# More buffers in each stage of the last group, and stretched pauses while two groups are emitted side by side

## The chip, the cores and the metric

The kernel runs on one core of a Trainium2 chip. The metric is the device time of that core in microseconds (us), smaller being better. The engines named below are TensorE (PE in the profile, with PEld for its weight loads), VectorE (DVE), ScalarE (ACT), GpSimd (POOL) and the queues that start transfers (SP is the one that starts nearly all of them here).

## The reference

The input x has 16 images of 32 channels and 128 by 128 pixels, all float32. Four layers follow one another, and each has the same frame; `_gn` is a group norm with 16 groups of two channels, without scale or shift:

```python
x = x + L0(_gn(x))      # a recurrence over the 128 columns: a row LSTM, 32 hidden channels
x = x + L1(_gn(x))      # adder convolution
x = x + L2(_gn(x))      # Hartley mode mixing
x = x + L3(_gn(x))      # edge operators and a small U-shaped stack of convolutions
```

L1 quantises its input and its 3x3 weights to 8 bits and takes, for each of 32 output channels, minus the sum of |patch − w| over all 288 taps.

L2 is this, with `dht2d` the Hartley transform along both axes (real minus imaginary part of the Fourier transform):

```python
xm = dht2d(x)[:, :, :32, :32]
z = einsum('bixy,ioxy->boxy', xm, yeven) + einsum('bixy,ioxy->boxy', flip(xm), yodd)
out = zeros((b, 32, 128, 128)); out[:, :, :32, :32] = z
return dht2d(out) / (128 * 128)
```

L3 applies five edge operators (Sobel, Scharr, Laplace, Roberts, Prewitt) to every channel with reflected borders. Each of the five results is normalised over all channels and pixels of its image. The 160 channels then go through this chain:

```python
y = maxpool2(conv3x3(edges, conv1)); y = maxpool2(conv3x3(y, conv2))
y = maxpool2(conv3x3(y, conv3));     y = conv3x3(y, conv4)
y = conv3x3(deconv2x2(y, deconv1), conv5)
y = conv3x3(deconv2x2(y, deconv2), conv6)
y = conv3x3(deconv2x2(y, deconv3), conv7)
return x_in * y                       # x_in: L3's normalised input
```

## The kernel before

The work goes in four groups of four images; four images times 32 channels fill the 128 partitions. The tensors between the layers (`x2` before L2, `x3` before L3, the modes `xm_d`, the mixed modes `z_d`, all in HBM) are written by one stage and read again by the next. `stage0` does the LSTM and takes the first 880 us. `rest` (from line 441) does everything else.

**Stage 1 and the weave.** `Differences.run` is the adder convolution. VectorE and ScalarE take the differences (lines 705 and 702), and TensorE sums them (line 592). It lasts until 5981 us. The layers L2 and L3 of groups 0, 1 and most of group 2 run inside it as a background: the class `After` holds them as one Python generator, and the class `Weave` steps this generator. The generator yields numbers. A positive number is TensorE's planned time of what was just emitted. A negative one is a pause: the weave emits nothing more of this generator until that much planned time has gone by. `SUMMED` is a wait of 4.5 us in the phase described next. `later(us, step)` puts a step off to a planned time; `done(v)` runs such a step at once if it has not run yet, since what follows needs it. All this happens while the program is written: the pauses set the order in which instructions are emitted, and nothing on the chip waits for a clock. In stage 1, `keep_order` then fixes that order on every engine.

**The drain.** When stage 1's emission is through, `end`, a copy of `After`, is made for group 3 (the last). It has the right side of SBUF, where stage 1's memory is free now, and four PSUM banks of its own. `drain` (line 403) then steps the two generators, what is left of group 2 and all of group 3, always the one with the lesser planned time, and when one has ended it goes on with the other, which is then `alone`. Each engine runs its instructions in its order; waits for data and for free buffers come from the tiles. Here `keep_order` is not applied, so the scheduler can still move instructions.

A tile pool with n buffers under one name lets n tiles of that name be alive; the next one waits until the oldest has been read for the last time. The same number decides here how many loads the code issues ahead. These are the stages of `After.work` for one group, with their lines:

- `forward`, line 974. Eight tiles `xh` of 1 MB (half an image's channels each) are loaded from `x2` (line 992), four of them ahead. VectorE takes the group means off (`centred`, line 1014). TensorE does the first transform (line 1061), transposes (line 1076) and does the second (line 1031); VectorE copies in between (lines 1065, 1020, 1035), and the modes `xm` go to HBM (line 1041).
- `modes`, line 1105. Per image the modes come back twice, as `xs` and flipped as `xw` (line 1114; four small loads), and VectorE adds the flipped ones (lines 1121 and 1128). This step is put off by 24 us.
- `mixing`, line 1139. Eight tables `mix` of 1 MB (line 1136), three ahead, and 512 small products on TensorE (line 1149); the results `z` go to HBM (line 1173).
- `back`, line 1176. `z` comes back (line 1198). Sixteen residual tiles `xr2` of 0.5 MB (line 1191), four ahead. TensorE does the inverse transforms (lines 1212 and 1257), VectorE adds the residual and takes its statistics (lines 1235 and 1237), and the sum goes to `x3` (line 1241).
- `frames` and `statistics`, lines 1280 and 1320. A ring of two frames `xp`, each 20 rows of the group's 128 planes, loaded in halves of 0.64 MB (line 1299) and normalised by ScalarE (lines 1305 to 1312). From eight frames TensorE builds Gram matrices (line 1345). VectorE multiplies these by five tables `gm` (loads in lines 1333 and 1412) and sums, 20 pairs of instructions (lines 1405 and 1406), which gives the variances of the five edge operators.
- `first_layers`, line 1445. Ten fold tables `v` (line 1458), three ahead, are scaled by these variances and added into one set of 3x3 weights `wf` (lines 1471 and 1473): conv1 with the five operators folded in.
- `conv1`, line 1603. The same frames are loaded again; the bias product (line 1617) comes first, then the borders (line 1633) and the main products (line 1661), and pooling.
- `small_layers`: conv2 to conv4 (TensorE line 1509, pooling on VectorE line 1586, the results' copy on ScalarE line 1600), and the deconvolutions, each composed with the convolution after it (lines 849 and 874).
- `last`, line 1717. Four units, each with a residual tile `xr` of 2 MB (line 1731; a ring of two), TensorE's last composed convolution (line 849), VectorE's scale and multiply-add (lines 1789 and 1752), and the stores to the output (line 1768).

At 5981 us group 2 stands in its Gram stage and group 3 at its beginning. In the profile, group 2's conv1 starts at 6202, its `last` runs from some 6720 to 6945; group 3's conv1 is alone from 6945 to 7035, and its small layers and `last` go to 7226.

Of the kernel before, what the change touches and what calls it, by code (L numbers as in the profile page):

```python
# [299 lines left out]
class Weave:  # L300
# [10 lines left out]
    def __init__(self, work):  # L311
# [3 lines left out]
        self.draining = self.alone = False  # L315
        self.finished, self.count, self.put_off, self.for_act, self.ends = -1, 0, [], [], {}

    def later(self, us, step):
        self.count += 1
        v = self.base + us, self.count, step  # L320
        self.put_off.append(v)
        return v
# [36 lines left out]
    def step(self):  # L359
# [16 lines left out]
        elif v < 0:  # L376
            wait = -v
        else:
            us = v
# [23 lines left out]
def drain(*weaves):  # L403

    live = list(weaves)
    for w in live:
        w.draining = True
    while live:
# [4 lines left out]
        if us is None:  # L413
            live.remove(w)
            for w in live:
                w.alone = True
# [24 lines left out]
def rest(nc, tc, cst, sel16, bias, m1, r1, a, d, out):  # L441


    with ExitStack() as ctx:
# [14 lines left out]
        end.spare = bg  # L459
        end.weave = Weave(end.work([NG - 1]))  # L460
# [442 lines left out]
class After:  # L903


    def __init__(self, nc, tc, side, sm, ps, cst, bias, a, d, stat, out):
        self.nc, self.tc, self.side, self.ps, self.cst, self.bias = nc, tc, side, ps, cst, bias
        self.a, self.d, self.stat, self.out = a, d, stat, out
        self.spare, self.banks = None, 0
        store = [d["up"][i] for i in range(3)]  # L910
# [63 lines left out]
    def forward(self, g):  # L974

        nc, tc, cst, d, weave = self.nc, self.tc, self.cst, self.d, self.weave
        x2, xm_d, z_d = d["x2"], d["xm"], d["z"]
        with self.pool("t_m") as mp:
# [6 lines left out]
            with self.pool("t_t") as tp, ExitStack() as rows:  # L985
                xp = rows.enter_context(self.pool("t_x", 4))
# [8 lines left out]
                xh = [load(n) for n in range(4)]  # L995
# [30 lines left out]
                def second(n):  # L1026
# [6 lines left out]
                    def out():  # L1033
                        xm = tp.tile([128, 4, M1], F32, name="xm", bufs=2)
# [45 lines left out]
                for n in range(10):  # L1080
                    if n < 7:
                        centred(n + 1)
                    if n < 8:
                        yield first(n)
                        if n + 4 < 8:
                            xh.append(load(n + 4))
# [10 lines left out]
                wp = rows.enter_context(self.pool("t_w", 3))  # L1097
                wt = [self.weights(wp, i) for i in range(3)]
# [6 lines left out]
    def modes(self, g, b, pool, xs, steps):  # L1105

        nc, weave, xm_d = self.nc, self.weave, self.d["xm"]
        xw = pool.tile([128, 16, 32], F32, name="xw", bufs=2)
# [30 lines left out]
    def mixing(self, g, xs, wp, wt):  # L1139
# [5 lines left out]
        for ky in range(M1):  # L1145
# [13 lines left out]
            if ky % 4 == 3 and 8 < ky < M1 - 1:  # L1159
# [16 lines left out]
    def back(self, g, load):  # L1176
# [3 lines left out]
        x2, x3, z_d = d["x2"], d["x3"], d["z"]  # L1180

        with self.pool("t_z") as zp_, self.pool("t_r", 4) as rp:
# [18 lines left out]
            for n in range(4):  # L1201
# [28 lines left out]
            def take_out(n, pf):  # L1230
# [9 lines left out]
                def store():  # L1240
                    nc.sync.dma_start(rows(n)(x3), xr[n])
                    ready[n + 4] = weave.later(6.0, lambda: reload(n + 4)) if n < 12 else None

                ready[n + 4] = weave.later(4.0, store)
# [26 lines left out]
            weave.later(7.0, lambda: [load(ch, half) for ch in range(2) for half in range(2)])  # L1271
# [8 lines left out]
    def frames(self, g, pool):  # L1280
# [5 lines left out]
        ring = [pool.tile([128, 20, W + 4], F32, name=f"xp{i}") for i in range(2)]  # L1286
        for t in ring:
            nc.vector.memset(t[:, :, 0], 0.0)
            nc.vector.memset(t[:, :, W + 3], 0.0)

        def parts(ch, half):
# [3 lines left out]
            return ring[ch % 2], lo, hi, ring[ch % 2][:, off : off + hi - lo, 2 : W + 2]  # L1295
# [673 lines left out]
```

## Time and profile before

| what | us |
|---|---|
| median of 3 runs | 7219.93 (7215.45 to 7227.18) |
| profiled execution, its own time | 7227.78 |
| its span in the profile | 7226.0 |
| `stage0` | 0 to 880 |
| stage 1, with the background | 880 to 5981 |
| drain | 5981 to 7226 |
| TensorE busy in stage 1 / in the drain | 4049.7 of 5101 / 960.1 of 1245 |
| VectorE busy in stage 1 / in the drain | 4739.3 of 5101 / 432.6 of 1245 |
| ScalarE busy in stage 1 / in the drain | 4801.5 of 5101 / 267.1 of 1245 |

The table's stretches come from the profile's busy times between two instants. In the listings below, a line such as `L1121` is a line of the kernel before, `out<-in` are tile names, and `<-` after a time names what ended the wait. In an order of time, the columns are the start in us, the duration, the engine (SPq is SP's queue), the line, the operation and its tiles; a bracket at the end holds the idle time before it. In a list of waits, the three numbers are total us, times, and the longest. A matmul's record can be missing here and there, and what is busy need not be at its peak.

### The profile page before, as it was taken

The page shows a single profiled execution, that of the slowest core. Times are in us where ns is not written, and L with a number is a line of the kernel's source. Part 1 is how long each engine was busy: PE and PEld are TensorE (multiplying, and loading weights), DVE is VectorE, ACT ScalarE, POOL GpSimd, SP SyncE. Part 2 cuts the span into 40 slices and gives each one's busy share as a digit, 9 for nine tenths or more (in the row PEclk, how much of TensorE's full clock was granted, in tenths as well). Part 3 has the DMA queues.
Part 4 walks back from the last instruction along what each step waited for, and adds up shares of the span by engine and source line. Part 5 has one row for each costly group of instructions (what it writes and reads, how often), then busy time and mean ns, then how long its engine had stood idle before and what let it go on. Part 6 is the DMA issues. An engine that isn't in the chain of part 4 may idle for free. (4 is left out here: it accounts for less than half of the span.)

```text
span 7226.0 us, 271421 instructions
## 1 busy us (share of the span) xinstructions
PE 5620.8 (78%) x127740; PEld 3002.2 (42%) x127740; DVE 5845.7 (81%) x7095; ACT 5502.0 (76%) x3100; POOL 52.1 (1%) x31
## 2 busy tenths in 40 slices
PE   4778567778877776998877786999775775797896
PEld 3666333333434342333334342333332443544574
DVE  7787699999989988999999998999997994234224
ACT  2555399999999988999999998999997992121222
POOL 0000000000000000000000000000000000000000
PEclk9899789999988898999989998999888997798897
DMA  8664211111132432221343343121243245352324
GB/s 310 228 205 148 79 64 57 53 58 50 44 108 85 140 100 72 62 76 43 76 121 109 109 122 99 60 66 51 64 122 89 79 128 140 95 157 83 87 58 104
DMA packets 374319, 722.57 MB, mean 100 GB/s; under 512 B 50896, under 2 KB 219856, under 8 KB 362320
## 3 DMA queue, kind: packets, MB, share of 16 engines
q1 hardware_dynamic: 372768, 704.58, 32.1%
q8 instruction: 999, 16.37, 1.0%
q14 instruction: 120, 0.98, 0.0%
q10 hardware_dynamic: 432, 0.64, 0.0%
HBM read 507.28 MB, written 164.32 MB: 93 GB/s over the span
## 5 line engine op out<-in xcount | busy, mean ns | idle before, releaser
L702 ACT ACTIVATE d_act<-q,neg 128x8192 f16<-128x8192 f16 (+1 forms) x631 | 4463.7, 7144 | 241.5 <-PE acc L592 192.6
L705 DVE TENSOR_SCALAR d_dve<-q,qw 128x8192 f16<-128x8192 f16 (+1 forms) x1673 | 3857.3, 2361 | 183.3 <-PE acc L592 141.1
L592 PE MATMUL acc<-d_dve,sel 128*32 128x512 f16 x26768 | 1863.1, 401 | 571.7 <-DVE d_dve L705 519.3
L592 PEld LDWEIGHTS <-sel 128*32 128x32 f16 x36864 | 1026.9, 100 | 2219.2 <-issue 1563.9
L1661 PE MATMUL acc<-xp,wf 32*32 32x512 f32 x25600 | 1034.1, 619 | 31.8 <-issue 26.5
L592 PE MATMUL acc<-d_act,sel 128*32 128x512 f16 x10096 | 725.0, 409 | 345.3 <-ACT d_act L702 333.6
L1661 PEld LDWEIGHTS acc<-xp,wf 32*32 32x32 f32 x25600 | 425.0, 104 | 401.1 <-issue 319.0
L622 PE MATMUL acc<-q,zero 128*32 128x512 f16 x7248 | 520.0, 399 | 0.0
L207 PE MATMUL pg<-h,wb 64*64 64x20 f32 (+15 forms) x4096 | 395.5, 319 | 105.7 <-DVE h L256 64.4
L1600 ACT ACTIVATE y<-pooled,b 32x128 f32<-32x128 f32 x488 | 195.1, 400 | 367.8 <-DVE pooled L1586 361.4
L849 PE MATMUL acc<-y,u_conv 32*32 32x256 f32 (+1 forms) x9728 | 356.2, 461 | 78.4 <-issue 49.3
L1305 ACT ACTIVATE xp<-xp,shift,stats 128x1280 f32<-128x1280 f32 (+1 forms) x128 | 182.9, 1434 | 276.4 <-DMA xp<-x_d 265.4
L244 ACT ACTIVATE gt<-pg,bias 128x20 f32<-128x20 f32 (+15 forms) x1024 | 316.8, 375 | 79.7 <-PE pg L207 72.8
L207 PE MATMUL pg<-e,wb 64*64 64x20 f32 (+15 forms) x4096 | 353.1, 315 | 16.5 <-DVE e L260 5.4
L207 PEld LDWEIGHTS pg<-h,wb 64*64 64x64 f32 x4096 | 248.2, 153 | 140.3 <-DVE h L256 90.0
L622 PEld LDWEIGHTS <-zero 128*32 128x32 f16 x7248 | 218.4, 101 | 201.8 <-issue 44.5
L207 PE MATMUL pg<-xn,wb 64*64 64x28 f32 (+61 forms) x4096 | 284.8, 303 | 11.6 <-ACT gt L244 3.8
L207 PEld LDWEIGHTS pg<-e,wb 64*64 64x64 f32 x4096 | 251.3, 156 | 92.5 <-DVE e L260 62.9
L1345 PE MATMUL acc<-xp 32*64 32x204 f32 (+3 forms) x8576 | 243.1, 343 | 33.9 <-ACT xp L1311 26.0
L255 ACT ACTIVATE th<-c 128x20 f32<-128x20 f32 (+15 forms) x256 | 81.3, 320 | 235.0 <-DVE c L253 233.6
L849 PEld LDWEIGHTS acc<-y,u_conv 32*32 32x32 f32 x9728 | 171.1, 110 | 189.8 <-issue 126.5
L1789 DVE TENSOR_SCALAR s<-acc,l_ms,l_one 128x512 f32<-128x512 f32 x128 | 101.4, 817 | 164.7 <-PE acc L849 164.7
(212 smaller groups left out, 4255.1 us busy)
## 6 DMA issues: line engine op xcount, KB each, us to landing
xr<-x_d SPq DMA_DIRECT2D x192, 512.0 KB
xp<-x_d SPq DMA_DIRECT2D x112, 640.0 KB
q<-q_d SPq DMA_DIRECT2D x32, 2145.0 KB
x_d<-xr SPq DMA_DIRECT2D x128, 512.0 KB
x_in<-in_x_dram SPq DMA_DIRECT2D x16, 2048.0 KB
res<-in_x_dram SPq DMA_DIRECT2D x64, 512.0 KB
xn<-in_xs_dram SPq DMA_DIRECT2D x64, 512.0 KB
xn<-xn SPq DMA_DIRECT2D x128, 256.0 KB
```

What stands on the lines that cost most here:

```text
L207: nc.tensor.matmul(bank[c][q][64 * pair : 64 * pair + 64, :, :width], wb[half, 4 * kind + KIND[q]].rearrange("p b o -> p (b o)"), v[half], ...
L244: nc.scalar.activation(gt[:, q, :, :n], bank[c][q][:, :, :n], AF.Tanh if q == G else AF.Sigmoid, bias=bias[:, KIND[q] : KIND[q] + 1],)
L592: self.nc.tensor.matmul(acc[k][32 * j : 32 * j + 32, :], self.sel16[:, i // 9, :], d[:, row : row + 4, c : c + W], start=first, stop=last,)
L622: self.nc.tensor.matmul(acc[k][32 * j : 32 * j + 32, :], self.zero, q[:, :4, :W], start=False, stop=False)
L702: nc.scalar.activation(dst, src, AF.Relu, bias=self.neg[:, i : i + 1])
L705: nc.vector.tensor_scalar(dst, src, self.qw[:, i : i + 1], 0.0, ALU.subtract, ALU.max)
L849: nc.tensor.matmul(acc[blk][32 * j : 32 * j + 32, o : o + rows * n], t[part, 4 * par + tap, :], src[part, top : top + rows, left : left + ...
L1305: nc.scalar.activation(v, v, AF.Identity, bias=self.shift3, scale=self.stats3[:, 1])
L1345: nc.tensor.matmul(gram[blk][j : j + width, at : at + n], xp[part, l, 2 + j : 2 + j + width], xp[part, rows, j : j + width + 4], start=sta ...
L1600: nc.scalar.activation(d, s, AF.Identity, bias=bj)
L1661: nc.tensor.matmul(acc[blk][32 * j : 32 * j + 32, :], tap_of("all", tap)[rows], xp[rows, 4 * j + kh : 4 * j + kh + 4, kw : kw + W], start= ...
L1789: nc.vector.tensor_scalar(s.rearrange("p r w b -> p b r w"), acc[blk].rearrange("p (b r w) -> p b r w", b=2, w=64), istd[:, blk : blk + 1] ...
```

## The change

`Weave` gets a factor `stretch`. It multiplies the delay of every `later` and every pause given as a negative number. It is 1 in stage 1, 1.5 in the drain while both generators live, and 1 again for the one that is left. The `SUMMED` wait of 4.5 us and the wait after `done` are not stretched. `mixing` drops its pause of 5 us in the drain.

`After` gets a table of buffer numbers, `buffers`, which sets both the pools' sizes and how many loads are issued ahead. `end` (group 3) gets a larger one. The other groups keep their numbers except for `xm`, which goes from 2 to 3. In the program that is built, everything up to the drain is the same on every engine but for this.

```diff
     def later(self, us, step):
         self.count += 1
-        v = self.base + us, self.count, step
+        v = self.base + us * self.stretch, self.count, step
...
         elif v < 0:
-            wait = -v
+            wait = -v * self.stretch
...
     for w in live:
-        w.draining = True
+        w.draining, w.stretch = True, 1.5
...
             for w in live:
-                w.alone = True
+                w.alone, w.stretch = True, 1.0
...
         end.spare = bg
+        end.buffers = {"t_x": 8, "xm": 8, "xw": 4, "t_w": 6, "t_r": 8, "frames": 4, "gm": 5, "e_v": 6, "l_x": 4}
...
         self.spare, self.banks = None, 0
+        self.buffers = {"t_x": 4, "xm": 3, "xw": 2, "t_w": 3, "t_r": 4, "frames": 2, "gm": 3, "e_v": 3, "l_x": 2}
...
-                xp = rows.enter_context(self.pool("t_x", 4))
+                xp = rows.enter_context(self.pool("t_x", ahead))
...
-                xh = [load(n) for n in range(4)]
+                xh = [load(n) for n in range(ahead)]
...
-                        xm = tp.tile([128, 4, M1], F32, name="xm", bufs=2)
+                        xm = tp.tile([128, 4, M1], F32, name="xm", bufs=self.buffers["xm"])
...
-                wp = rows.enter_context(self.pool("t_w", 3))
-                wt = [self.weights(wp, i) for i in range(3)]
+                wp = rows.enter_context(self.pool("t_w", self.buffers["t_w"]))
+                wt = [self.weights(wp, i) for i in range(self.buffers["t_w"])]
...
-        xw = pool.tile([128, 16, 32], F32, name="xw", bufs=2)
+        xw = pool.tile([128, 16, 32], F32, name="xw", bufs=self.buffers["xw"])
...
-            if ky % 4 == 3 and 8 < ky < M1 - 1:
+            if ky % 4 == 3 and 8 < ky < M1 - 1 and not weave.draining:
                 yield -5.0
...
-            for n in range(4):
+            for n in range(ahead):
                 residual(n)
...
-        ring = [pool.tile([128, 20, W + 4], F32, name=f"xp{i}") for i in range(2)]
+        ring = [pool.tile([128, 20, W + 4], F32, name=f"xp{i}") for i in range(self.buffers["frames"])]
...
-                    load((ch + 2) % 8, half)
-                    if ch + 2 < H // 16:
-                        ready[ch + 2, half] = normalise(ch + 2, half, 18.0)
+                    load((ch + ahead) % 8, half)
+                    if ch + ahead < H // 16:
+                        ready[ch + ahead, half] = normalise(ch + ahead, half, 18.0)
...
-        gm = [pool.tile([128, GRAM], F32, name="gm", bufs=3) for _ in range(3)]
-        for k in range(3):
+        gm = [pool.tile([128, GRAM], F32, name="gm", bufs=tables_ahead) for _ in range(tables_ahead)]
+        for k in range(tables_ahead):
             nc.sync.dma_start(gm[k], self.a["gram"][:, k])
...
-        with self.pool("e_v", 3) as pool:
+        with self.pool("e_v", self.buffers["e_v"]) as pool:
...
-        with self.pool("l_y") as yp, self.pool("l_x", 2) as xp:
+        with self.pool("l_y") as yp, self.pool("l_x", self.buffers["l_x"]) as xp:
...
-            xr = [load(0), load(1)]
+            xr = [load(unit) for unit in range(ahead)]
```

In `back`, `statistics`, `conv1` and `last` the indices of what is reloaded follow the same numbers (`ahead` in the place of 4, 2, 2 and 2). In `last` of group 3 all four units are loaded at its start, so nothing is reloaded.

## The prediction

> **What bounds the kernel now.** I read the span first, then cut the end of the run into stretches, then asked each stretch for its waits and its order of time. The last matmuls of stage 1 run at 5980 us. From there to 7226 us only the two weaves are left: what is left of group 2, and all of group 3. The built programs of both kernels are the same on every engine up to that point, so all that follows concerns the last 1245 us. The first fence is the page's first line; the second is the table of stretches (us, then busy time of each engine, the granted TensorE clock, the DMA share, GB/s).
>
> ```profile
> span 7226.0 us, 271421 instructions
> ```
>
> ```profile
> 5981.00:6225.00 244.00, 116.48 (x3518) 92.23 (x3502) 99.66 (x234) 23.34 (x41) 4.23 (x5) 0.63 0.55 156
> 6225.00:6600.00 375.00, 356.68 (x10506) 192.68 (x10489) 93.61 (x267) 103.38 (x223) 0.66 (x3) 0.99 0.36 103
> 6600.00:6700.00 100.00, 60.93 (x2005) 39.93 (x1999) 70.60 (x174) 3.48 (x7) 0.00 (x0) 0.61 0.25 78
> 6700.00:6945.00 245.00, 213.00 (x6881) 140.05 (x6877) 71.23 (x131) 68.71 (x119) 0.00 (x0) 0.92 0.39 88
> 6945.00:7035.00 90.00, 88.91 (x2719) 71.76 (x2713) 16.23 (x60) 19.80 (x46) 0.21 (x1) 0.98 0.21 51
> 7035.00:7226.00 191.00, 124.11 (x4357) 85.63 (x4325) 81.25 (x164) 48.29 (x80) 0.00 (x0) 0.77 0.41 99
> ```
>
> The first number after the comma is the length, the second the busy time of TensorE. Its idle time is the first minus the second: 127.5, 18.3, 39.1, 32.0, 1.1 and 66.9 us, together 285. Nothing that only reorders work can win more than that. Where TensorE is busy 95% (the second stretch) a buffer or a pause has nothing to win. So I ask what ends the idle time in the first, the third and the last stretch. The waits of the first stretch (total, times, longest):
>
> ```profile
> ACT xp L1305 <- DMA xp<-x_d: 129.9, 12, 25.9
> ...
> DVE xw L1121 <- DMA xw<-xm_d: 51.1, 8, 12.4
> ...
> PE acc L1149 <- DVE xs L1128: 30.3, 1, 30.3
> ...
> PE acc L1617 <- DVE wf L1473: 25.1, 1, 25.1
> ```
>
> The first is group 2's Gram stage, fed by two frames. The second is group 3's: VectorE, which works in order, stands in front of the mode additions until their small loads land, and group 2's Gram sums (L1405) stand behind them. The third and fourth are the results: mixing begins late, and conv1 of group 2 waits 25 us for its weights. VectorE's order of time shows one of these waits and the Gram sums behind it:
>
> ```profile
> 6121.26 0.17 DVE L1121 COPY xw<-xs 64x32 f32<-64x32 f32 x1 [12.39 <-DMA xw<-xm_d]
> ...
> 6127.82 0.59 DVE L1405 TENSOR_TENSOR es_w<-acc,gm 128x420 f32<-128x420 f32 x1
> ```
>
> SP's queue at the start of the stretch shows what the extra loads will have to pass:
>
> ```profile
> 5983.57 1.67 SPq L992 DMA_DIRECT2D xh<-x_d  x1
> 5985.34 11.29 SPq L1299 DMA_DIRECT2D xp<-x_d  x1
> 5996.84 8.78 SPq L992 DMA_DIRECT2D xh<-x_d  x3
> 6005.73 26.84 SPq L1299 DMA_DIRECT2D xp<-x_d  x6
> ```
>
> In the third stretch TensorE waits for group 2's pooling, which stands behind 18 of group 3's 20 Gram pairs on VectorE; in the last, VectorE waits twice for a reload of the residual:
>
> ```profile
> PE acc L1509 <- DVE pooled L1586: 17.1, 1, 17.1
> ```
>
> ```profile
> 7174.46 1.42 DVE L1752 SCALAR_TENSOR_TENSOR xr<-xr,l_ms,s 128x512 f32<-128x512 f32 x2 [10.15 <-DMA out_dram<-xr]
> ...
> 7201.50 1.42 DVE L1752 SCALAR_TENSOR_TENSOR xr<-xr,l_ms,s 128x512 f32<-128x512 f32 x2 [11.77 <-DMA out_dram<-xr]
> ```
>
> **What the Trainium skill says.** "DMA: Bandwidth & Descriptors", section "Queues, rings and completion order": on each DMA engine descriptors are consumed in ring order, so a small load issued after large ones starts behind them. The trace agrees: the one frame load behind the first xh held SP 11.29 us, against 0.36 us where nothing is queued. "TensorE: Matmul & The Clock Gate", part 1: an idle array falls to half clock. The granted clocks 0.63 and 0.61 of the two idle stretches against 0.99 agree, so idle time removed there also speeds what is left. "Runtime: NRT & Kernel Launch", section "Instruction fetch mechanics": an engine fetches blocks of 256 instructions by DMA. The edge matmuls (L1633) pause 1.9, 3.0, 4.7, 2.2 and 2.5 us, mostly after each 128 matmuls and their 128 weight loads, with nothing to wait for; the change leaves those pauses.
>
> **The change, part by part.** Only group 3 gets buffers; group 2 keeps its two frames, three weight tables and two residual units. I go by the order in the built program of the changed kernel.
>
> 1. *Eight xh loads at once.* Four more loads of 1 MB each pass two of group 2's frame loads on SP. The frame loads of 0.64 MB behind them landed some 2.1 us apart in the trace (they were normalised at 6015.4, 6017.7, 6019.7), 300 GB/s; the first four xh and their neighbours took about 31 us for 6.5 MB, 210 GB/s. So the four cost between 13 and 20 us, and that is how much later group 2's next frame lands. VectorE's new order puts the edge copies of these late frames ahead of group 3's statistics and first centring, and all eight centrings (2.29 us each) ahead of the first transposed copy. I count the first transpose at 6068 against 6040.6: 27 us late. From there nothing waits for xh any more (7.7 us before).
> 2. *xm, xw, and pauses of 1.5.* The additions of images 2 and 3 now stand behind nearly all the Gram sums rather than ahead. The additions of images 0 and 1 still stand where they wait, some 9 and 13 us by the same landings as before (8.5 to 14 us from issue). Eight passes of 4.5 us (the trace's rate where nothing stalls), less what overlaps, and these two waits bring the first Gram sum to about 6121 (6127.8 before); 40 operations of 0.59 to 0.62 us and some 4 us of group 3's copies between them bring the end to 6150 (6171 before, since 15 us of waits fell between).
> 3. *Six mixing tables ahead.* 6 MB are now issued before the last two images' small loads, 3 MB before. At 300 GB/s the backlog lasts until about 6145, the last two pairs land at about 6152 and 6161, and the addition ends at 6163. TensorE's new order has the Gram pair first, then 384 of 512 mixing products, then conv1. Mixing (31 us for all, so 24 for 384) then runs beside the 22.5 us of weight folding instead of before it. Folding ends about 7 us after the Gram chain's 6163, plus 22.5 less what is folded meanwhile: conv1 starts at about 6188 against 6201.9. The 128 products left over go in pieces of 16 between conv1's and cost 3 to 6 us. The pause that is dropped from mixing costs nothing: no engine waits for it. Sum: 14 less 6, **8 us won**.
> 4. *Four frames, eight residuals in the inverse transform.* They fall in 6225 to 6600, where TensorE is 95% busy: 18.3 us of idle is all there is, I take **2 us**. Cover gone, the frame waits would cost what they cost group 2. In the new order conv1 of group 2 is nearly through when group 3's Gram stage begins, which then shares TensorE with conv2; four frames are what lets it keep up.
> 5. *gm and v.* Five Gram tables ahead take two waits off SP that held group 2's conv3 weights to 6611; six fold tables take off most of the 3.6 us of VectorE waits (1.6, 1.0 and shorter) in group 3's folding. On VectorE, pooling of conv2's second half now stands behind 12 of the Gram pairs rather than 18: 6 pairs of 1.25 us, 7.5 us off the wait of 17.1. Against it, conv4's evictions (4.5 us) now stand ahead of the last folding. conv1 of group 3 starts about as long after its Gram stage, but up5's first round is done by then, some 8 us of TensorE work. **8 us won**.
> 6. *Four residual units.* Units of the last stage end at 7137.9, 7159.6, 7186.6 and 7213.9: 21.7, then 27.0 and 27.4. With every unit loaded ahead the last two take 21.7 like the second: 10.9 us. The 4 MB more at the start meet instruction fetches there (the trace has a pause of 4.5 us at 7116 during the first loads); I take 3 us off. **8 us won**.
> 7. *Pauses from 6700 to 7035.* The waits here are instruction fetches and the work is the same: nothing.
>
> Sum: 8 + 2 + 8 + 8 = 26 us. The profiled execution took 7227.8 us (span 7226.0 and 1.8 around it): 7202. The three runs have their median at 7219.9, 7.9 lower, so I forecast **7194**.
>
> **The rivals.** *Slower: the flood of loads.* If the seven extra megabytes (four xh, three mixing tables) come at 210 GB/s, the frames are 20 us late, the last two images' loads land past 6180, and folding begins only after them: conv1 at 6215, 13 us later than before, with mixing still to be finished, and up to 10 us more where the inverse transform's input waits. With small gains elsewhere the sum is +20: **7240**. It decides from the point where mixing starts later than 6185. For it: 129.9 us of ScalarE's waits are for group 2's frames already. Against it: the Gram sums fill VectorE meanwhile. *Nothing to be had.* TensorE is 89% busy from 6225 to 7035 (719.5 of 810 us), and what is won ahead is lost to longer waits behind: **7220**. For it: fetch pauses move with the work; against it: the last stage's two waits have no other owner. *Everything at once.* Mixing fills the whole 25.1 us, the third stretch loses 20 of its 39 us of idle, the last 11 and the returned clock does the rest: about 60 less, **7160**. *The pauses do not do what they say*: they only order instructions, and where a queue is in order and its data are there, an instruction runs early whatever its due time; then stretching alone is worth nothing, which the sums above assume already.
>
> **How the numbers follow.** My forecast has 0.45, everything at once 0.15, nothing 0.2, slower 0.2. About 0.2% (14.4 us) is what a measurement of this kernel can tell from no change: faster is below 7205.5, slower above 7234.4. Faster takes all of the 0.15 and 0.43 of the forecast: 0.58. Slower takes 0.19. The rest is the same. The range 7150 to 7240 reaches over the gain's rival and to the slower rival's middle; the forecast's own is 7175 to 7215.
>
> **What would show it.** Step 1: first transpose near 6068. Step 2: first Gram sum near 6121, with no wait for xw of over 5 us inside them but the last. Step 3: the wait before L1617's matmuls gone or under 5 us, conv1 near 6188. Step 5: the 17 us wait near 10. Step 6: no wait of the last stage for a reload, the stage 8 us shorter. It is wrong if mixing begins past 6185, or if the stretch of 95% grows.

## The result, and the profile after

The changed kernel's four first runs have their median at 7237.6 us, against 7223.6 for the kernel before; the ratio is 1.0016, with a 95% interval from 0.9996 to 1.0036. A longer comparison (21 runs, below) makes it 1.0014, from 1.0008 to 1.0021: about 10 us slower. The forecast was 26 us less. The profiled execution took 7237.96 us:

```profile
span 7236.0 us, 271378 instructions
```

One thing has to come first, since it decides how the two profiles are compared. Stage 1, whose instructions are the same, did not end at the same time: the last adder sum on TensorE (line 592 before, 595 after; the lines after are some 3 to 11 higher) ended at 5980.3 us before and at 5972.2 after (to within 0.3 us), and in the profiles below anywhere from 5967 to 5996. So I count from that instant and call the rest of the span **the drain**. It took 1245.7 us before and 1263.8 after: 18 us more, although the span grew by 10 only. The table of stretches, with the first one starting at stage 1's end:

```profile
5972.00:6225.00 253.00, 123.83 (x3702) 97.48 (x3698) 98.98 (x228) 23.33 (x41) 4.05 (x4) 0.65 0.46 138
6225.00:6600.00 375.00, 350.97 (x10526) 191.40 (x10537) 96.72 (x282) 110.25 (x237) 0.87 (x4) 0.99 0.43 126
6600.00:6700.00 100.00, 62.08 (x1851) 35.09 (x1821) 72.65 (x177) 7.54 (x11) 0.00 (x0) 0.62 0.15 49
6700.00:6945.00 245.00, 211.30 (x6724) 133.47 (x6706) 60.45 (x116) 59.07 (x109) 0.21 (x1) 0.94 0.37 86
6945.00:7035.00 90.00, 88.86 (x2657) 73.96 (x2656) 19.58 (x60) 17.29 (x36) 0.00 (x0) 0.98 0.12 27
7035.00:7236.00 201.00, 130.15 (x4522) 87.00 (x4513) 82.85 (x171) 48.34 (x80) 0.00 (x0) 0.78 0.42 94
```

TensorE's idle time (first number less second): 129.2, 24.0, 37.9, 33.7, 1.1, 70.9, together 297 where it was 285. What was to shrink has not: the first stretch and the last are idle longer than before. The waits of the first stretch:

```profile
ACT xp L1313 <- DMA xp<-x_d: 100.0, 9, 26.3
DVE sides L1384 <- ACT xp L1319: 54.6, 5, 18.1
DVE xw L1126 <- DMA xw<-xm_d: 39.2, 8, 10.2
...
DVE zs L1171 <- PE acc L1154: 9.9, 1, 9.9
...
PE acc L1627 <- DVE wf L1482: 6.9, 1, 6.9
```

The waits for xw fell from 51.1 to 39.2 us and the wait of conv1 for its weights from 25.1 to 6.9 (under 5 was forecast). In exchange VectorE waits 54.6 us for ScalarE's frames (39.0 before), and the wait for mixing's results (9.1 us in two waits before, 9.9 in one now) has moved into the middle of folding. SP's queue and VectorE's order of time show where:

```profile
6000.86 12.89 SPq L997 DMA_DIRECT2D xh<-x_d  x4
6013.88 32.56 SPq L1307 DMA_DIRECT2D xp<-x_d  x7
```

```profile
6025.27 0.28 DVE L1384 COPY sides<-xp 128x16 f32<-128x16 f32 x2 [16.52 <-ACT xp L1319]
...
6039.00 11.10 DVE L1019 TENSOR_TENSOR xh<-xh,mr 128x2048 f32<-128x2048 f32 x5
...
6164.96 1.85 DVE L1482 SCALAR_TENSOR_TENSOR wf<-v,ops,wf 128x1152 f32<-128x1152 f32 x2 [1.51 <-DMA v<-fold_d]
6176.67 1.06 DVE L1171 COPY zs<-acc 128x256 f32<-128x256 f32 x2 [9.86 <-PE acc L1154]
```

The four extra xh loads hold SP for 12.89 us with seven frame loads of group 2 behind them; VectorE's copy of a frame's borders waits 16.52 us for the late frame (1.31 us before), and group 3's statistics and all centrings stand behind that copy. Later, in the middle of folding, VectorE stands 9.86 us for the first half of mixing. In the third stretch the wait for pooling is shorter, as forecast:

```profile
PE acc L1518 <- DVE pooled L1595: 10.4, 1, 10.4
```

In the last stage no reload is waited for any more. What took its place is in the transfers, here from 7090 us to the end (forty equal slices; each digit is the busy share in tenths, the second row GB/s), first before, then after:

```profile
DMA  0099999920000079910039999400399993003994
GB/s 5 5 241 206 224 219 218 212 43 5 5 5 5 5 152 220 220 34 5 5 76 234 211 218 335 180 5 5 81 236 216 211 355 149 0 0 72 208 230 106
```

```profile
DMA  0009999999999920019940049910008970000994
GB/s 4 4 4 229 211 215 218 217 217 212 218 220 211 215 46 4 4 37 207 236 113 4 4 103 211 231 38 4 4 4 186 238 159 4 0 0 20 212 229 113
```

The full-rate burst at the start of the stage lasts eleven slices of 3.65 us in place of six of 3.4. The first unit is done 52.5 us after the first residual load (39.9 before); the three others then take 69.5 us (76.1). The last stage, from conv2 of group 3 to the end, is 199.0 us long (193.2).

### The profile page after: what moved, and what is told of

Its sections match the earlier page's. It is cut to its first block, busy times and chain, and to the rows that moved or that the text cites. A ratio compares the mean times of both kernels' runs of the same rounds, so it can differ in the third digit from the quotient of the medians.

```text
span 7236.0 us, 271378 instructions
## 1 busy us (share of the span) xinstructions
PE 5639.8 (78%) x127740; PEld 2999.5 (41%) x127740; DVE 5844.1 (81%) x7099; ACT 5499.1 (76%) x3100; POOL 56.8 (1%) x31
## 3 DMA queue, kind: packets, MB, share of 16 engines
q8 instruction: 999, 16.37, 0.9%
```

## The experiments

Each run has its time as a ratio to the kernel before on the same chip, and a profile. From the profile I give the drain, the start of conv1 of group 2 after stage 1's end, and the time from conv2 of group 3 to the end.

| run | time ratio, 95% interval | drain, us | conv1 of group 2 | conv2 of group 3 to end |
|---|---|---|---|---|
| before (first, again) | 1.0001 (0.9993 to 1.0009) | 1245.7, 1248.5 | 221.6, 222.7 | 193.2, 194.0 |
| changed (first, again) | 1.0014 (1.0008 to 1.0021) | 1263.8, 1260.2 | 219.0, 219.6 | 199.0, 201.9 |
| s1 | 1.0053 (1.0040 to 1.0066) | 1281.8 | 239.8 | (overlaps) |
| p15 | 1.0009 (1.0001 to 1.0017) | 1262.1 | 211.5 | 193.3 |
| lx2 | 1.0014 (1.0006 to 1.0022) | 1248.4 | 221.1 | 197.1 |
| tx4 | 0.9997 (0.9985 to 1.0009) | 1241.7 | 206.1 | 201.0 |
| zs_act | 1.0019 (1.0011 to 1.0027) | 1252.3 | 218.8 | 203.2 |
| lx_late | 1.0011 (1.0003 to 1.0018) | 1244.1 | 219.8 | 196.5 |
| tx4_lx2 | 0.9992 (0.9980 to 1.0004) | 1238.2 | 207.7 | 195.6 |
| tx4_lx2_s1 | 1.0025 (1.0016 to 1.0034) | 1275.9 | 228.1 | (overlaps) |
| tx4_lx2_tw3 | 0.9990 (0.9981 to 0.9998) | 1239.4 | 212.6 | 193.3 |
| gram_only | 1.0013 (1.0002 to 1.0024) | 1261.4 | 231.0 | 197.2 |
| lx4_only | 1.0008 (0.9999 to 1.0016) | 1247.7 | 219.6 | 196.7 |
| early3 | 1.0011 (1.0003 to 1.0019) | 1254.6 | 213.5 | 183.6 |
| before_early3 | 1.0020 (1.0011 to 1.0028) | 1255.3 | 225.5 | 183.4 |
| p15_apart | 1.0012 (1.0005 to 1.0018) | 1259.7 | 211.0 | 192.3 |

The rows stand in four sets, each measured together: down to p15, to lx_late, to gram_only, and the last four. Within a set drains may be compared, though each row is one profile. Across sets the ratio decides: lx2 and lx_late, whose edits touch the last stage only, reach conv2 of group 3 after 1051 and 1047 us, and the changed kernel, in the first set and before it, after 1058 and 1065. "Overlaps" means that four products of that conv2 stand inside conv1; from the rest to the end it is 196 us in both.

**Both kernels again.** No edit.

> The kernel before once more, to learn how far the drain's own length (from the end of the last adder sum on TensorE to the end of the span; 1245.7 us in the profile of before) repeats. If the drain repeats within 5 us, the difference of 18 us between the two first profiles (1245.7 and 1263.7) belongs to the change; if it wanders by 10 us or more, it may be chance. Time: within 0.3% of 7223.

> The changed kernel once more, five rounds. Drain 1263.7 us in its first profile; within 5 us of that if the loss is the change's own, and near 1250 if the first profile was chance. Last stage: first unit done some 52 us after the first residual load, and the three others in 69 to 70 us together.

The drain repeats within 3 and 4 us; 12 us lie between the two in this pair, 18 in the first. The loss is the change's own, and its places repeat too: conv1 of group 2 at 219.6, first unit 52.1 us after its first load and 69.9 for the others.

**Buffers without stretched pauses (s1), and pauses without buffers (p15).**

```diff
-        w.draining, w.stretch = True, 1.5
+        w.draining, w.stretch = True, 1.0      # s1
...
-        end.buffers = {"t_x": 8, "xm": 8, ...}
+        pass                                   # p15
```

> All the buffers, no stretched pauses (factor 1.0 throughout). Theory P (the pauses cost: they put the mixing behind conv1 of group 2, so the inverse transform starts 32 us late): mixing's last product before conv1 of group 2 begins, the inverse transform starts within 25 us of that as before, drain 1240 to 1252. Theory L (the loads issued ahead cost, wherever the instructions stand): drain 1258 to 1270, the first transposes still 20 us late, and what is won by earlier mixing lost to late loads.

> The stretched pauses and mixing without its pause, with the buffers of before in the last group. Theory P: mixing again runs between conv1's products and ends some 40 us after conv1 of group 2 begins, drain 1255 to 1265. Theory L: the late instructions cost nothing as TensorE has conv1 to do, drain 1240 to 1250. Both: the last stage as before, its first unit done about 40 us after the first residual load, and reload waits of 10 and 12 us.

Neither theory holds as written. Without the factor 1.5 the buffers cost 38 us (0.53%), more than the whole change; the factor without the buffers costs some 6 us (0.09%; 15 us in the drain of its profile); together they cost 10. Both runs leave out mixing's pause of 5 us, as the change does, and p15 keeps the third buffer of xm; neither of the two was tried by itself. So the stretched pauses do something, contrary to the prediction's last rival: with the larger buffers they save 28 us. In s1 most of mixing stands ahead of the Gram sum in TensorE's order, as in the kernel before, and with the late start the sum is at 209.9 us (191.3 before, 168.2 with the change) and conv1 18 us later than before. With the pauses the Gram sum goes first. What p15 loses comes late: from conv1 of group 3 to the end of group 2 TensorE is idle 57.1 us of 252.8 (39.6 of 270.9 before). Two of these pauses stand side by side in TensorE's order of time:

```profile
6703.02 1.53 PE L1643 MATMUL acc<-sides,wf 32*32 32x32 f32 x128 [7.86 <-issue]
6712.52 1.53 PE L1643 MATMUL acc<-sides,wf 32*32 32x32 f32 x128 [7.97 <-issue]
```

"issue" means that the engine waited for no tile and no semaphore that the profile shows. The busy times for the same 21 us (TensorE first) say what else went on: 4 MB of residuals came in for group 2's last stage, with the DMA engines fully busy at 208 GB/s.

```profile
6692.00:6713.00 21.00, 3.64 (x331) 3.26 (x319) 5.81 (x9) 5.35 (x8) 0.00 (x0) 0.61 1.00 208
```

Between two pauses lie 128 matmuls, each with its weight load: 256 instructions. That is the block in which, by the Trainium skill, "Runtime: NRT & Kernel Launch", section "Instruction fetch mechanics", an engine fetches its instructions by DMA. The page calls the cost "mostly hidden". Here it isn't. So a third theory, F: instruction fetches wait behind data bursts, and a burst costs TensorE time wherever it falls.

The traces let the first half of F be checked, since they list these transfers too. The page of the kernel before has a queue `q8 instruction: 999, 16.37, 1.0%`, that is 999 transfers in 16.37 MB, or 16 KB each. At 256 instructions each they are 255,744; TensorE's matmuls and weight loads are 255,480, so I take this queue to be TensorE's. In the 21 us above, two blocks came:

```profile
q8 instruction: 2, 0.03, 0.8%
```

They landed at 6701.56 and 6710.88 us, 9.2 and 9.3 us after the block before each, and the matmuls above begin 1.5 and 1.6 us after that. The transfers took 1.3 us once they had begun: they began late. In the whole drain before, 38 of the 40 such pauses of at least 1 us end between 1.0 and 2.2 us after a block has landed, times that make up some 22% of the drain. Where under 20 GB/s moved, a block landed 3.8 us after the one before it (median of 131), and where over 180 GB/s moved, after 6.5 us (median of 50). A pause is what the work in a block can't cover: these 128 matmuls take 1.53 us.

**Two residual units (lx2), four loaded late (lx_late), and four in the kernel before (lx4_only).** In lx2 the ring is 2. lx_late keeps four buffers:

```diff
-            xr = [load(unit) for unit in range(ahead)]
+            xr = [load(unit) for unit in range(2)]
...
-                following[unit] = weave.later(10.0, lambda: reload(unit)) if unit + ahead < 4 else None
+                following[unit] = None
+                if ahead == 4 and unit < 2:
+                    xr.append(load(unit + 2))
...
```

lx4_only is the kernel before with `l_x` at 4 for the last group.

> The changed kernel with the residual ring of the last stage back at two units. If the four units loaded at once cost what the last stage lost (first residual load to the end of the run 122.0 us in both profiles of the change, 116.7 and 118 before): first unit done 40 us after the first load (52 with the change), the run ends 116 to 118 us after that load, drain 1256 to 1258 against 1262. If the first unit is late for another reason (the order of instructions): it stays at 50 to 52, and the reload waits of 10 and 12 us come on top, drain 1270.

> The changed kernel with four buffers in the last stage, but only two units loaded at its start; units 2 and 3 are loaded right behind the issue of the stores of units 0 and 1, into buffers that are free, so they need not wait for these stores to land. If the burst of 8 MB is what makes the first unit late: first unit done 40 us after the first load, no wait of VectorE over 3 us for a residual, the others in 66 to 70 us together, the run ends 107 to 111 us after the first load (122.0), drain 1248 to 1251. If loads behind the stores come too late: waits of 3 to 8 us at units 2 and 3, end at 114 to 118.

> The kernel before with four residual units in the last stage of the last group, and nothing else of the change. If the burst of 8 MB by itself costs more than the two reload waits: first unit done 52 us after the first load (39.9 and 40.1), the three others in 66 to 71 us together (76 to 77), the run ends 120 to 124 us after the first load less than 7 us of tail, that is 135 to 137 to the very end of the span (129.6 and 130.9 before); drain 1250 to 1254; time 1.0004 to 1.001. If the prediction's 8 us are right where nothing else is changed: first unit 41 to 44, to the end 121 to 124, time 0.9989.

The first unit is done after 39.8 us in lx2 and 38.9 in lx_late, 51.7 in lx4_only: the burst of 8 MB costs 12 us there, whatever else is changed. Late blocks show most of it. Between the first load and the end of the first unit, TensorE has three pauses of 4.4 to 5.1 us with no wait shown in each of the three profiles that load four units at once (both of the changed kernel, and lx4_only), and one, of 4.2 to 4.8 us, in each of five that load two (both of the kernel before, lx2, lx_late and tx4_lx2). Each follows a block of instructions that landed 8.6 to 9.4 us after the one before it. In all TensorE is idle 20 to 21 us there, and 11 to 12.5 with two units: some 8 of the 12 us. Two of the changed kernel's three:

```profile
7134.84 0.68 PE L852 MATMUL acc<-y,u_conv 32*32 32x256 f32 x8 [4.82 <-issue]
...
7143.79 1.81 PE L852 MATMUL acc<-y,u_conv 32*32 32x256 f32 x40 [4.44 <-issue]
```

The three others take 77.3, 80.2 and 68.0 us. In lx2 the two reload waits are back (11.7 and 11.4 us), and the stage is 4 to 6 us below those of its set with four units loaded at once (197.1 against 201.0 and 203.2); in time lx2 can't be told from the changed kernel. lx_late missed its number: VectorE waits for no reload, but the third unit alone takes 32.7 us, as TensorE pauses 5.2, 3.0, 4.1 and 3.1 us with no wait shown, each time until 1.3 to 1.5 us after a block of instructions has landed, while 2 MB of stores and 2 MB of loads go together. In the kernel before, the four units cost 3 us of the stage and 0.08% of the time, with an interval that just takes in no change. The prediction's 8 us are nowhere to be had.

**Four xh loads (tx4), and mixing's result copied by ScalarE (zs_act).**

```diff
-"t_x": 8
+"t_x": 4                                       # tx4
...
-                nc.vector.tensor_copy(dst, zv[y][...])
+                copy_z = nc.scalar.copy if weave.draining else nc.vector.tensor_copy
+                copy_z(dst, zv[y][...])                # zs_act
```

> The changed kernel with four xh loads ahead in place of eight; all else kept. If the eight loads at once are what makes the start late: first transpose of group 3 60 to 66 us after stage 1's end (85.5 and 86.1 with the change), the Gram sum 10 to 15 us earlier than 168 to 169, conv1 of group 2 at 208 to 213 (219 to 220), drain 1252 to 1256. If the six mixing tables, or the wait for mixing's first half in the middle of VectorE's folding, set the start of conv1: transposes earlier, conv1 still at 217 or later, drain 1260 to 1264.

> The changed kernel with mixing's results copied out of PSUM by ScalarE in the drain, not by VectorE; TensorE's order is the same. If the wait of 9.9 us for mixing's first half, in the middle of the ten foldings, is what holds conv1 of group 2: folding takes 22 us (31.3), conv1 starts when mixing's 384 products end, 210 to 213 us after stage 1's end (219 to 220), and 6 to 8 us of TensorE's idle time are gone, drain 1254 to 1257. If the fold tables are late for their own sake: folding 29 to 31 us, conv1 at 217 or later, drain unchanged at 1260 to 1264.

tx4 came as the first reading said: first transpose at 62.2 us (85.4), conv1 of group 2 at 206.1 (208 to 213 was forecast), TensorE's idle time before it 104.8 us (120.4 in zs_act), drain 10.6 us below zs_act, and a time 0.22% below it. In VectorE's order of time the border copy that waited 16.52 us in the changed kernel now waits 1.97, and the centrings behind it begin 52.4 us after stage 1's end in place of 66.8:

```profile
6007.05 0.28 DVE L1384 COPY sides<-xp 128x16 f32<-128x16 f32 x2 [1.97 <-ACT xp L1319]
...
6020.75 8.90 DVE L1019 TENSOR_TENSOR xh<-xh,mr 128x2048 f32<-128x2048 f32 x4
```

zs_act did what it was made for and won nothing. Folding takes 22.5 us (31.3), yet conv1 starts at 218.8, because the 384 mixing products that stand ahead of it now end no earlier. They take 30 us in place of 25, with four pauses of 5.9 us together (one of 1.2 us in the changed kernel), for the same busy time (23.7 us). The seven fold tables, no longer held back, are issued in 13.2 us in place of 22.2, and 250 GB/s move during mixing in place of 171. All four pauses end as above, 1.4 to 1.5 us after a block of instructions has landed, and these blocks came 4.9 to 6.9 us apart. Two of them:

```profile
6176.92 4.05 PE L1154 MATMUL acc<-xs,mix 128*32 128x8 f32 x128 [1.34 <-issue]
...
6188.52 3.81 PE L1154 MATMUL acc<-xs,mix 128*32 128x8 f32 x120 [2.71 <-issue]
```

So the wait of 9.9 us stood beside another limit of nearly the same length: beside the tables that came sooner, TensorE's instructions came later. tx4 shows the eight loads to be the cause of the late start.

**Both bursts gone, with pauses (tx4_lx2), without (tx4_lx2_s1), and with three mixing tables (tx4_lx2_tw3).** The edits are the numbers in `end.buffers` ("t_x": 4, "l_x": 2, and "t_w": 3 in the third) and the factor 1.0 in the second.

> The changed kernel with both bursts gone: four xh loads ahead and two residual units, all else of the change kept. If the two losses are separate, they add: conv1 of group 2 at 206 us after stage 1's end as with four xh loads alone, first unit of the last stage 39 to 40 us after its first load, drain some 4 to 5 us below 1241.7, time 0.9990 of before. If the gain at the start is lost later whatever the last stage does: 0.9997 to 1.0005.

> The same without stretched pauses. If the burst of xh loads alone made the version without pauses slow (1.0053): conv1 of group 2 at 220 to 225 (239.8), time 0.999 to 1.002. If the larger buffers without pauses cost by themselves, by letting group 3 push itself between group 2's instructions: conv1 at 220 to 225 too, but conv1 of group 2 ends 40 us or more later than before (587), and the time stays at 1.003 or more.

> As the first of these, with three mixing tables ahead in place of six. If six tables delay the small loads behind them: the last two images' additions 4 to 8 us earlier, mixing begins at 168 to 171 (174.9 with six), conv1 of group 2 at 203 to 206, drain 2 to 4 us less. If six tables are what feeds mixing: mixing stops for its fourth and later tables, 384 products take 28 us or more (24 to 25), conv1 at 208 to 214.

The first came within 4 us of its parts: 207.7, first unit 40.0, time 0.9992. Without the pauses conv1 is at 228.1 (220 to 225 was forecast) and conv1 of group 2 ends at 634 (567 with them, 587 before), as the second theory said; the time is 1.0025 (1.003 or more was forecast). So larger buffers without stretched pauses, and with mixing's pause left out, cost by themselves, even without the bursts. From conv1 of group 3 to the end of group 2 this version is idle 61.4 us of 359.9. Three mixing tables came as neither theory said (mixing 3 us earlier at 172.8 and no slower, but conv1 5 us later at 212.6) and make no clear difference: 0.9990, 0.1% below the kernel before, can't be told from the 0.9992 of six tables.

**The Gram stage's buffers alone (gram_only).** The kernel before with `frames` 4, `gm` 5 and `e_v` 6 for the last group, and the change's three buffers for xm.

> The kernel before with only the Gram stage's buffers of the change (four frames, five gm, six fold tables), no stretched pauses. If they are worth the 8 us that the prediction gave them: end of group 3's Gram products to its conv1 55 us (63.3 and 63.6 before), time 0.9989. If that stage gives back what it wins: 55 us there, and as much more between its conv1 and the end; time 0.9997 to 1.0005. If they only let group 3's matmuls push ahead of group 2's: group 2's conv1 ends 20 us or more later, time 1.002 or more.

The stage itself came out even shorter than forecast, 52.6 us from the end of group 3's Gram products to its conv1 (63.3), though TensorE's idle time in it fell by 3 us only; the rest is work that now stands elsewhere. But conv1 of group 2 ends at 614 in place of 587, from conv1 of group 3 to its conv2 it takes 392.2 us (368.1 and 372.5), and the time is 1.0013. Some 9 us were lost before conv1 of group 2 already. SP's queue shows what differs there. Nine loads that the kernel before issues after 6200 us, four residuals xr2 and the five tables gm, stand in front of five of group 2's frame loads:

```profile
6005.02 3.77 SPq L1197 DMA_DIRECT2D xr<-x_d  x4
6008.83 3.86 SPq L1342 DMA_DIRECT2D gm<-in_gram_dram  x5
```

The border copy that waits 1.31 us before now waits 9.78 us. That is the kind of delay that the eight xh loads cause, but these loads weren't tried apart. From that point to the end the drain is 1030.4 us (1024.1 and 1025.8): nothing is won there either.

**Residual units loaded during conv1 (early3, before_early3), and one burst split (p15_apart).** For the first two:

```diff
+            if ch in self.early:                # (2, 4, 6)
+                self.units.append(self.unit(g, self.lp, len(self.units), out[3]))
...
+    def unit(self, g, pool, unit, behind=None):
+        xr = pool.tile([128, 4, 8 * W], F32, name="xr3")
+        if behind is not None:
+            self.nc.vector.tensor_copy(xr[:, 0, :1], behind[:, 0, :1])
+        ...four loads
```

In p15_apart, which is p15 with one more edit, group 2's second unit is loaded in this way behind the first half of unit 0.

> The changed kernel with four xh loads ahead, three frames, four residuals xr2 and four fold tables, and three residual units of the last stage loaded one by one during conv1 of group 3 (a one-column copy of the pooled result of its 3rd, 5th and 7th frame into the unit's tile holds each load back until then). If bursts in front of instruction fetches are what made the last stage slow: no load at its start but the composed weights, TensorE's pauses for nothing shown there down from 27 to 32 us to 12 to 18, conv2 of group 3 to the end of the span 172 to 180 us (201 and 202 with the change, 193 and 194 before), conv1 no more than 4 us longer, time 0.9965 to 0.998. If the pauses belong to the many small matmuls whatever the queues carry: pauses 25 us or more, conv2 to the end 185 or more, time 0.9985 or more.

> The kernel before, and three residual units loaded in the same way during conv1 of group 3; no other buffer and no pause is changed. If bursts are the cause: conv2 of group 3 to the end 172 to 180 us (193 and 194), all before conv2 as before within 4 us, drain 1228 to 1236, time 0.9975 to 0.9987. If not: 185 or more, time 0.9993 to 1.0005.

> The version with stretched pauses and the buffers of before, with the first two residual units of group 2's last stage loaded apart: the second one only after the first half of unit 0. In the version without this, two pauses of 7.9 and 8.0 us fell into the borders of conv1 of group 3, while 4 MB came in. If the burst made them: one of them is gone or both are 5 us or less, and 6 to 14 us less idle from conv1 of group 3 to the end of group 2 (57.1). If they belong to the fetches alone: two pauses of 7 us or more remain.

The last stage became 10 us shorter than before in both (183.6, 183.4), and what lies ahead of it 13 to 21 us longer: conv1 to conv2 of group 3 takes 385.7 and 389.1 us (368.1 and 372.5). Both lost. In both, four residuals xr2 also go out among group 2's first frames, as in gram_only, though no edit asks for it; conv1 of group 2 is later than without (225.5 against 221.6 and 222.7; 213.5 against 206.1 and 207.7). Pauses went with the bursts: in before_early3, SP's queue and TensorE's order of time for conv1 alone, where the kernel before is idle 1 us in 97:

```profile
6961.49 4.51 SPq L1742 DMA_DIRECT2D xr<-x_d  x4
...
7024.06 2.41 SPq L1742 DMA_DIRECT2D xr<-x_d  x4
```

```profile
6975.62 56.51 PE L1675 MATMUL acc<-xp,wf 32*32 32x512 f32 x1662 [5.01 <-issue]
7035.96 15.02 PE L1675 MATMUL acc<-xp,wf 32*32 32x512 f32 x406 [3.82 <-issue]
```

Each of these two loads of 2 MB is met by one pause, of 5.01 and 3.82 us, and in front of each a block of instructions landed 9.4 us after the one before it. Between the two TensorE runs 1662 matmuls in 56.5 us with no pause. From 6976 to 7024 the DMA engines are 12% busy, and twelve blocks came, one in 4 us:

```profile
q8 instruction: 12, 0.20, 1.7%
```

128 of these matmuls take some 4.4 us, longer than a block on its way. So the same lateness of a block costs nearly 8 us beside the borders' short matmuls and 4 to 5 beside these. And not every burst costs: a frame's two loads, 1.15 MB at 250 to 300 GB/s, fall into the stretch without a pause. In p15_apart one of the two long pauses is gone (8.13 and 2.76 us in place of 7.86 and 7.97), but only 3.5 us of idle with it, not 6 to 14, and its time is no better than p15's. In early3 TensorE's unexplained pauses from conv2 of group 3 on are still 32 us (44 in the changed kernel, 38 before), not 12 to 18. The blocks say what these are. I take what moved, on average, between a block's landing and that of the block before it. Of the 38 us before, 26.7 follow by 1.0 to 2.2 us a block with over 100 GB/s and 8.8 one with under 20; in the changed kernel it is 31.7 and 7.2 of 44, in early3 18.5 and 12.6 of 32. With the loads gone from there, the stores and the last load remain, and the short matmuls, whose work doesn't last until the next block even without a burst. So the first half of F holds: blocks come late beside bursts. The second does not hold as written: what a late block costs depends on the work that TensorE has at hand.

## Why the prediction was wrong

By its steps, in TensorE's idle time, each side as the mean of two profiles:

- **Step 1, eight xh loads.** First transpose forecast 27 us late; 25.2 measured in the first pair of profiles (85.5 and 60.3 us after stage 1's end). The size was right. What failed is what followed from it: I let the delay vanish in the slack of later steps. tx4 shows that 13 to 15 us of it came through to conv1 of group 2 (206.1, and 218.8 to 221.1 in the rest of its set).
- **Steps 2 and 3.** First Gram sum forecast at 141 us after stage 1's end, measured 138.6; Gram chain's end 170 and 168.2; mixing 183 and 187.2. Then conv1: 208 and 219.0. I had put folding beside mixing and overlooked, in VectorE's order, that the copies of mixing's first half stand in the middle of it (9.9 us; zs_act shows that nothing is won by moving them alone). And TensorE had done 10 to 12 us less work before conv1 than before, where I took 3 to 6. Idle before conv1 of group 2 went from 112.6 to 120.8 us: 8.2 lost, where 8 were to be won. Without the four extra loads it is 104.8 and 105.0: close to the 8 us of the forecast, and step 1 took twice that away.
- **Step 4.** Idle from there to the end of group 3's Gram products: 30.7 and 30.8. Nothing, where I took 2.
- **Step 5.** The wait went from 17.1 to 10.4 us (10 forecast), and idle in that stage from 30.2 to 28.2 us: 2 won, not 8. The work that moved ahead met 4.5 and 5.3 us of other waits. gram_only shows the same: the stage 11 us shorter, 3 of them idle, and more than that lost elsewhere.
- **Step 6.** Forecast 8 won; the stage became 5.8 and 7.9 us longer. The two reload waits went, but the last two units took 24.1 and 24.8 us, not 21.7, so the three units behind the first gained 6.6 to 7.3 us, not 10.9; and the first came 12.3 us later. I had the collision of loads and instruction fetches and its example, and took 3 us for it: the term was mis-sized by a factor of four. My example was one pause of 4.5 us; with four units three such pauses stand there, where two units have one.
- **Step 7.** Nothing forecast between 6700 and 7035. From conv1 of group 3 to its conv2 idle went from 42.7 to 44.1 us: as forecast, nearly.
- **The stretched pauses.** The last rival takes them for nothing, by an argument on order alone, and the sums took that over. s1 says that beside the larger buffers they save 28 us, and p15 that alone they cost 6.

The sum of the idle terms is 8.2 + 0 − 2 + 1.4 + 4.8 = 12.4 us; the drain is 15 us longer, the rest being busy time of TensorE. That the two terms named, steps 1 and 6, are the loss is shown by tx4_lx2: with both bursts gone the ratio goes from 1.0014 to 0.9992. The rival with the flood had one of the two culprits. That its number (7240) lies so near is partly luck: it came from a gap of 20 us, and 10 were measured. Its deciding point, mixing past 6185 (205 us after stage 1's end), was not reached: mixing began at 187. It was the frames that were late, and all that VectorE keeps in order behind them.

## What to carry to other kernels

A buffer that lets a load go earlier also puts it in front of something: list what stands behind it in the queue, and what an in-order engine holds back for that. Count what is won in a stage where the end is set, not in the stage: three gains here (folding, the Gram stage, the last stage) were real and were given back elsewhere. Where many short matmuls run, count the instructions too: a burst of loads there makes their blocks late. Moving the burst beside longer matmuls made each pause shorter here (5.0 and 3.8 us in place of 7.9), but early3 and before_early3 as a whole still lost. Between two executions of the same instructions, count from a common instant; here the shared part wandered by more than the effect.

## What the runs showed of the hardware

- The same instructions at the start (`stage0` and stage 1, some 6 ms, alike but for xm's buffers) ended between 5967 and 5996 us over eighteen profiles, and between 5974 and 5996 in the four of the first set.
- A TensorE pause with no wait shown ends, in 38 of 40 cases of at least 1 us in the drain before, 1.0 to 2.2 us after a block of 256 instructions has landed.
- Such a block landed 3.8 us after the one before where under 20 GB/s moved (median), and some 9 us after it in front of the longest pauses, beside loads of 2 to 8 MB. A pause was 7.9 us where the block's work took 1.5 us, and 5.0 or 3.8 where it took some 4.4.
- The pauses with no wait shown made up 122 us of the 1246 us drain before, 125 to 128 in the changed kernel, and 143 to 149 in s1, p15 and tx4_lx2_s1.
